# A graph network layer on one core: the window rows asked for earlier, five groups of source rows fetched by SyncE, more groups on ScalarE, narrower last blocks

## The chip, the cores and the metric

The kernel runs on one NeuronCore of one Trainium2 chip. The metric is the device time of one execution in microseconds. A run is timed three times; the median counts. One further execution is recorded by the hardware profiler, and all rows below come from such a record.

## The reference

12,500 nodes with 128 features each, 400,000 edges sorted by their destination, 32 features per edge. Cut to what matters:

```
h   = relu(layernorm(x))
pre = concat(h[src], h[dst], edge_attr) @ w1 + b1            # one row per edge
m   = relu(pre) @ w2 + b2
agg = segment_sum(m, dst)                                    # one row per node
gi, gh = agg @ w_ih + b_ih, h @ w_hh + b_hh
r, z = sigmoid(i_r + h_r), sigmoid(i_z + h_z)
n   = tanh(i_n + r * h_n)
out = x + (1 - z) * n + z * h
```

## The kernel before

w1 is split in three. `A = h @ w1[0:128]` and `B = h @ w1[128:256] + b1` are computed once per node and kept in DRAM; the node states also stay in SBUF, transposed, as `hT_all`. An edge then needs a row of `A` (by its source), a row of `B` (by its destination) and a product with the last 32 rows of w1.

**Groups and units.** The edges are cut into 391 groups (`k`) of eight tiles of 128 edges, 1024 edges each. A group is worked in two units, so the main loop runs over 782 units (`u`), and unit `u` emits for several groups at once: the product for unit `u + 3`, the addition for unit `u + 2`, the sum over destinations for unit `u`.

**The product (`pre`, L644).** Since the edges are sorted, a tile's destinations lie in a window of 32 nodes. `RW` is a tile of 128 rows: twice 32 window rows of `B`, and the edge weights; there are four of them (`RW[k % 4]`). `window_rows(k)` (L575) brings the two sets of 32 rows with two DMAs of SyncE. `L` holds the one-hot matrix of the places (made on VectorE, L545) and the edge features; `fetch(q)` brings it for two groups with two DMAs of SyncE, `L<-in_dstP` (L533, 256 KB, each of two source rows repeated for 32 partitions) and `L<-in_eaP` (L536, 256 KB). There are three `L` buffers.

**The source rows.** For most groups POOL gathers the rows of `A` into a buffer `G` with eight indirect DMAs (L152), as far ahead as 12 buffers allow. VectorE adds them to the product and applies the relu in one instruction (L668). For some groups, spread evenly, the sources are brought "by hand": `one_by_one` copies single columns of `hT_all` into `HE`, on ScalarE (L905, 24 groups) or on VectorE (L912, two columns per instruction, 26 groups), with node numbers loaded into registers (L899, 16 or 32 per load); TensorE multiplies them with w1a into the same sum (L655), and ScalarE does the relu (L675). `run_jobs` spreads the copies of a job evenly over the units between two groups.

**The sums.** `seg` (L688) adds the rows of one group by destination, `take` (L696) copies the sums, and after each block of 14 groups `node` computes the gates for 512 nodes; `last_node` does so for the last block, step by step in the last units.

**The order of the work** is written out by hand: each engine runs its instructions in the order in which the main loop emits them. A unit has four phases; `other(phase)` places the jobs and the small work. Of SyncE, a unit emits, if its number is even, the `fetch` of every second group; in phase 2 of an odd unit `window_rows(k + 3)`; besides these the stores of `B` (L237), the loads and stores of the node blocks (L703, L800) and index tiles (L107, L118). SyncE's DMAs take eight semaphores in turn.

Of the kernel before, what the change touches and what calls it, by code (L numbers as in the profile page):

```python
# [23 lines left out]
GRP = 4  # L24
# [5 lines left out]
V = 32  # L30
# [2 lines left out]

BP, BW = 14, 512
DMIN = 320
BLOCKS = [(BP * b, BP, BW) for b in range(27)] + [(378, 5, 256), (383, 8, 320)]
NB = len(BLOCKS)
NW = 27
LEAST = [DMIN] * 28 + [16]
QP = 2  # L40
W = 96
NT = -(-N // 128)
NFULL = N // 128
BAT = (4,) + (8,) * 11 + (NFULL - 92, 1)
RAW = 10
GBUFS = 12
BATCH = 512
AHEAD = 32
ROOM = V * (AHEAD - 2)
PLACE = 20  # L50
CH = PLACE * PAIR
LOAD = {"act": 16, "dve": 32}
PIECE = 128
STEP = {"act": 4, "dve": 8}
SPREAD = {"dve": 26, "act": 24}
START = {"dve": 16, "act": 4}
NR = 12672

H_AT = 16512
# [3 lines left out]
def tile_gnn(ctx: ExitStack, tc: tile.TileContext, x, src, srcT, dstT, dstP, eaT, eaP, w1, b1, w2T, b2,  # L63
# [25 lines left out]

    mode, order = {}, {m: [] for m in SPREAD}  # L90
    for m, n in SPREAD.items():
        lo, hi = START[m] // 2 + 2, NP - {"dve": 9, "act": 6}[m]
        for i in range(n):
            k = lo + int((i + 1) * (hi - lo) / n)
            while k in mode:
                k += 1
            mode[k] = m
            order[m].append(k)
# [75 lines left out]
    nc.vector.memset(brow, 0.0)  # L174
    b1b = const.tile([128, D], F32, name="b1b")
    base_d = at[96:97, :NP - 1]
    by_hand = [k for m in ("act", "dve") for k in order[m]]
    NJ = len(by_hand)
    zrow = const.tile([1, BW], BF16, name="zrow")
    nc.vector.memset(zrow, 0.0)  # L180
    RW = [const.tile([128, 2, D], F32, name=f"RW{i}") for i in range(4)]
# [556 lines left out]
    def node(b):  # L738
        w = BLOCKS[b][2]
        g0, xb, offs = block_start(b)  # L740
        pt = ps1.tile([128, 512], F32, name="nd")[:, :w]
        pd = ps1.tile([128, 512], F32, name="misc")[:, :w]
        nc.vector.tensor_copy(dcol[:2 * V, :len(offs)], sums[:, :len(offs), D])
        zero(pt)
        for i in range(len(offs)):
            sum_of(b, pt, offs, i)
        zero(pd)
        for i in range(len(offs)):
            degree_of(b, pd, offs, i)
        d = step_of(b)  # L750
        yield 1
        carry(b, TOT, pt, d)
        carry(b, DEG[0:1, :], pd[0:1, :], d)
        yield 1
        g = nc.tensor.value_load(blk_i[0:1, b:b + 1], min_val=0, max_val=N - w)
        hT = hT_all[:, bass.ds(g, w)]

        def gate(name, i, with_h, with_s):
            c = slice(i * D, (i + 1) * D)
            ci = slice(2 * D, 3 * D) if i == 3 else c  # L760
            pg = ps1.tile([128, 512], F32, name=name)[:, :w]
            nc.tensor.matmul(pg, brow[:, c], DEG[:, :w], start=True, stop=False)  # L762
            if with_h:
                nc.tensor.matmul(pg, whh_s[:, ci], hT, start=False, stop=not with_s)
            if with_s:
                nc.tensor.matmul(pg, w2ih[:, ci], TOT[:, :w], start=False, stop=True)  # L766
            return pg

        pr = gate("nd", 0, True, True)
        yield 1  # L770
        r = temp(w)
        nc.scalar.activation(r, pr, AF.Sigmoid)  # L772
        ph = gate("misc", 3, True, False)
        yield 1
        t = temp(w)
        nc.vector.tensor_tensor(t, r, ph, op=ALU.mult)
        pi = gate("nd", 2, False, True)
        yield 1
        nc.vector.tensor_tensor(t, t, pi, op=ALU.add)
        pz = gate("misc", 1, True, True)  # L780
        yield 1
        nc.scalar.activation(t, t, AF.Tanh)
        z = temp(w)
        nc.scalar.activation(z, pz, AF.Sigmoid)
        yield 1
        gv = nc.vector.value_load(blk_i[0:1, b:b + 1], min_val=0, max_val=N - w)
        q = r
        nc.vector.tensor_tensor(q, hT_all[:, bass.ds(gv, w)], t, op=ALU.subtract)
        yield 1
        nc.vector.tensor_tensor(q, q, z, op=ALU.mult)  # L790
        yield 1
        nc.vector.tensor_tensor(q, q, t, op=ALU.add)
        yield 1
        po = ps1.tile([128, 512], F32, name="nd")[:w // 4, :]
        for i in range(4):
            nc.tensor.transpose(po[:, i * D:(i + 1) * D], q[:, i::4], ident)
        yield 1
        nc.vector.tensor_tensor(xb, xb, po.rearrange("p (i f) -> p i f", i=4), op=ALU.add)
        yield 4 if b < NW - 1 else 1
        nc.sync.dma_start(out[bass.ds(g0, w), :].rearrange("(p i) f -> p i f", i=4), xb)  # L800

    def last_node():
# [16 lines left out]
            sum_of(b, pt, offs, i)  # L819
        yield  # L820
        carry(b, DEG[0:1, :], pd[0:1, :], d)
        for i in range(n - 4, n - 1):
            yield
            sum_of(b, pt, offs, i)
        yield

        def gate(pool, name, i, h_too):
            c = slice(i * D, (i + 1) * D)
            pg = pool.tile([128, 512], F32, name=name)[:, :w]
            nc.tensor.matmul(pg, brow[:, c], DEG[:, :w], start=True, stop=False)  # L830
            if h_too:
                ci = slice(2 * D, 3 * D) if i == 3 else c
                nc.tensor.matmul(pg, whh_s[:, ci], hT, start=False, stop=i == 3)
            return pg

        def finish(pg, i):
            nc.tensor.matmul(pg, w2ih[:, i * D:(i + 1) * D], TOT[:, :w], start=False, stop=True)

        pr = gate(ps1, "nd", 0, True)
        ph = gate(ps1, "misc", 3, True)  # L840
        yield
        pi = gate(ps2, "seg", 2, False)
        pz = gate(ps2, "pre", 1, True)
        yield
        sum_of(b, pt, offs, n - 1)
        carry(b, TOT, pt, d)
# [44 lines left out]
        return h_bytes[:, bass.ds(v - H_AT, 4)]  # L891

    def one_by_one(m, k):
        et = {"act": ET.Activation, "dve": ET.DVE}[m]
        r = by_hand.index(k)
        hand[k] = pj.tile([128, PAIR * 128], F32, name=f"HE_{m}")
        he = hand[k].bitcast(U8)
        for e0 in range(0, PAIR * 128, LOAD[m]):
            _, vals = nc.values_load_multi_w_load_instructions(  # L899
                at[r:r + 1, e0:e0 + LOAD[m]], engines=[et], min_val=H_AT, max_val=H_AT + 4 * (N - 1),  # L900
                skip_runtime_bounds_check_because="src holds numbers of nodes")
            if m == "act":
                for i, v in enumerate(vals):
                    e = e0 + i
                    nc.scalar.copy(he[:, e * 4:e * 4 + 4], column(v))  # L905
                    if i % STEP[m] == STEP[m] - 1:
                        yield
                continue
            if e0 % PIECE == 0:
                both = pj.tile([128, PIECE // 2, 4], U16, name="both")  # L910
            for i in range(0, LOAD[m], 2):
                nc.vector.scalar_tensor_tensor(both[:, (e0 % PIECE + i) // 2, :], column(vals[i + 1]),  # L912
                                               256.0, column(vals[i]), op0=ALU.mult, op1=ALU.add)
                if i % STEP[m] == STEP[m] - 2:
                    if (e0 + i + 2) % PIECE == 0:
                        p0 = e0 + LOAD[m] - PIECE
                        nc.vector.tensor_copy(  # L917
                            he[:, p0 * 4:(p0 + PIECE) * 4].rearrange("p (n c b) -> p n c b", c=2, b=4),
                            both.bitcast(U8).rearrange("p n (b c) -> p n c b", c=2))
                    yield  # L920

    jobs = {}
    for m, kl in order.items():
        start = START[m]
        for k in kl:
            end = 2 * k - 4
            jobs.setdefault(start, []).append((m, k, end - start))
            start = end
    live = {}

    PH = 4
# [26 lines left out]
    gathers(0)  # L958
    for q in range(3):
        fetch(q)  # L960
    for k in range(3):
        window_rows(k)


# [30 lines left out]
                    left.pop(0)  # L995

    last = last_node()
    LAST_STEPS = (NU - 8, NU - 6, NU - 5, NU - 4, NU - 2, NU - 1)

    for u in range(NU):  # L1000
        k, h = divmod(u, 2)
        gathers(u)
        if h == 0:
            if k % QP == 0:
                fetch(k // QP + 3)
            if k and k == BLOCKS[block(k)][0]:
                nodes_left.append([node(block(k) - 1), 2 if k < BLOCKS[-1][0] else 1])
            if k % PLACE == 1:
                indices(k // PLACE + 2)
            if k % PLACE == 5:  # L1010
                place(k // PLACE + 1)
                dst_tile(k // PLACE + 2)
            if k == NP - 20:
                check_windows()
        if u == min(START.values()) - 2:
            nc.vector.tensor_scalar(at[:NJ, :], at[:NJ, :], 4.0, float(H_AT), op0=ALU.mult, op1=ALU.add)

        def other(phase):
            run_jobs(u, phase)
# [1 line left out]
                batch_product(batch_due(k), wide[1], p3, "xb", 2)  # L1021
            if h == 1 and phase == 1 and batch_due(k):
                batch_store(batch_due(k))
            if h == 1 and phase == 2:
                window_rows(k + 3)
            if h == 0 and phase == 3:
                take(k - 1)
            if phase == 3:
# [11 lines left out]
        other(3)  # L1040
    for it, _ in nodes_left:
        run(it)
    next(last)
    next(last)
    take(NP - 1)
    run(last)

# [168 lines left out]
```

## Time and profile before

| What | Value |
|---|---|
| Median of 3 runs | 3548.33 us (3529.08 to 3559.73) |
| The profiled execution | 3567.68 us, its span 3565.9 us |
| Granted TensorE clock | 0.783 |
| TensorE busy | 2409.1 us (68%) |
| VectorE busy | 2266.0 us (64%) |
| ScalarE busy | 2661.4 us (75%) |
| POOL busy | 2614.4 us (73%) |
| Gathers from A on POOL | 2648 |
| SyncE: `RW<-B`, `L<-in_dstP`, `L<-in_eaP` | 782, 196 and 196 DMAs |
| DMA | 337.57 MB, mean 95 GB/s |

Busy time leaves out register loads, waits and the issuing of DMAs, so an engine may be occupied far more than its share says; SyncE shows none at all. A row of the waits names the instruction that waited, what it waited for, the total in us, the number of times and the longest. A row of a timeline gives the start, the length, the engine (a q behind it: its queue), line, operation, tiles and count, and in brackets the idle time before it. A row of a source view gives the smallest, median and largest duration in ns.

### The profile page before, as it was taken

The page shows a single profiled execution, that of the slowest core. Times are in us where ns is not written, and L with a number is a line of the kernel's source. Part 1 is how long each engine was busy: PE and PEld are TensorE (multiplying, and loading weights), DVE is VectorE, ACT ScalarE, POOL GpSimd, SP SyncE. Part 2 cuts the span into 40 slices and gives each one's busy share as a digit, 9 for nine tenths or more (in the row PEclk, how much of TensorE's full clock was granted, in tenths as well). Part 3 has the DMA queues.
Part 4 walks back from the last instruction along what each step waited for, and adds up shares of the span by engine and source line. Part 5 has one row for each costly group of instructions (what it writes and reads, how often), then busy time and mean ns, then how long its engine had stood idle before and what let it go on. Part 6 is the DMA issues. An engine that isn't in the chain of part 4 may idle for free. (4 is left out here: it accounts for less than half of the span.)

```text
span 3565.9 us, 80442 instructions
## 1 busy us (share of the span) xinstructions
PE 2409.1 (68%) x13224; PEld 1536.2 (43%) x13224; DVE 2266.0 (64%) x16484; ACT 2661.4 (75%) x25007; POOL 2614.4 (73%) x2734
## 2 busy tenths in 40 slices
PE   6567666675776676577667766765766676667768
PEld 6444444443444444344444443443444344434435
DVE  7656666666656666666566666666666666666664
ACT  5497778768777778787678688768876887796782
POOL 7677777777777777777777777777777777777770
PEclk8788877777777877777777878778777788787868
DMA  6433333333333333333333333333333333333431
GB/s 198 100 87 93 93 94 93 90 96 93 92 89 93 92 92 95 93 96 92 94 94 96 92 95 95 93 93 96 95 91 95 94 98 96 96 91 91 95 94 31
DMA packets 188489, 337.57 MB, mean 95 GB/s; under 512 B 65118, under 2 KB 108701, under 8 KB 187967
## 3 DMA queue, kind: packets, MB, share of 16 engines
q0 software_dynamic: 87200, 178.76, 21.5%
q1 hardware_dynamic: 100623, 153.56, 15.8%
q14 instruction: 412, 3.38, 0.3%
q8 instruction: 110, 1.80, 0.2%
q10 hardware_dynamic: 144, 0.07, 0.0%
HBM read 311.87 MB, written 20.27 MB: 93 GB/s over the span
## 5 line engine op out<-in xcount | busy, mean ns | idle before, releaser
L152 POOL DMA_INDIRECT G<-A,src_i x2648 | 2540.1, 959 | 839.6 <-issue 761.9
L905 ACT COPY HE_act<-hT_all 128x4 uint8 x24576 | 2470.3, 189 | 57.9 <-issue 38.3
L644 PE MATMUL pre<-RW,L 128*128 128x256 f32 x3128 | 1149.9, 495 | 1079.9 <-DMA RW<-B 827.5
L912 DVE SCALAR_TENSOR_TENSOR both<-hT_all 128x4 uint16 x13312 | 1138.0, 153 | 970.6 <-issue 961.4
L644 PEld LDWEIGHTS pre<-RW,L 128*128 128x128 f32 x3128 | 672.9, 240 | 1379.5 <-issue 669.8
L688 PE MATMUL seg<-RB,OH 128*32 128x129 f32 x6250 | 592.3, 319 | 0.0
L668 DVE CUSTOM_DVE_ANT_0 RB<-pre,G 128x512 f32<-128x512 f32 x662 | 448.5, 677 | 133.3 <-PE pre L644 98.8
L675 ACT ACTIVATE RB<-pre 128x512 f32<-128x512 f32 x120 | 70.7, 589 | 481.6 <-PE pre L655 481.3
L688 PEld LDWEIGHTS seg<-RB,OH 128*32 128x32 f32 x6250 | 326.8, 123 | 208.5 <-issue 159.0
L545 DVE TENSOR_SCALAR L<-L,node_of 64x512 f32<-64x512 int32 x383 | 187.2, 489 | 6.1 <-DMA L<-in_dstP 5.9
L772 ACT ACTIVATE gt<-nd 128x512 f32<-128x512 f32 (+1 forms) x28 | 16.5, 588 | 228.8 <-PE nd L766 228.8
L596 DVE TENSOR_TENSOR OH<-dloc,wide 128x256 f32<-128x256 f16 (+1 forms) x392 | 158.9, 406 | 0.5 <-issue 0.3
L696 DVE COPY sums<-seg 64x129 f32<-64x129 f32 x391 | 108.1, 277 | 17.2 <-PE seg L688 17.2
L683 PEld LDWEIGHTS <-zrow 1*64 1x64 bf16 x391 | 41.4, 106 | 143.4 <-issue 134.8
L683 PE MATMUL seg<-zrow 1*64 1x129 bf16 x391 | 99.4, 254 | 2.3 <-DVE sums L696 2.2
L917 DVE COPY HE_dve<-both 128x512 uint8<-128x512 uint8 x208 | 93.2, 448 | 7.1
L713 PE MATMUL nd<-spot,sums 64*128 64x40 f32 x766 | 94.2, 285 | 0.0
L713 PEld LDWEIGHTS nd<-spot,sums 64*128 64x128 f32 x766 | 90.7, 193 | 6.2 <-issue 6.1
L152 POOL DMA_INDIRECT G<-in_x,src_i x77 | 72.8, 945 | 24.4 <-issue 23.2
L655 PEld LDWEIGHTS pre<-w1a,HE_dve 128*128 128x128 f32 x416 | 75.6, 226 | 9.1
L655 PEld LDWEIGHTS pre<-w1a,HE_act 128*128 128x128 f32 x384 | 73.7, 239 | 9.1
L762 PE MATMUL nd<-DEG,brow 34*128 34x512 f32 (+1 forms) x112 | 75.0, 755 | 0.9 <-DVE DEG L727 0.9
(193 smaller groups left out, 1414.3 us busy)
## 6 DMA issues: line engine op xcount, KB each, us to landing
L<-in_dstP SPq DMA_DIRECT2D x195, 256.0 KB
L<-in_eaP SPq DMA_DIRECT2D x195, 256.0 KB
G<-A,src_i POOLq DMA_INDIRECT x2648
RW<-B SPq DMA_DIRECT2D x782, 16.0 KB
xb<-in_x SPq DMA_DIRECT2D x27, 256.0 KB
out<-xb SPq DMA_DIRECT2D x27, 256.0 KB
xs<-in_x SPq DMA_DIRECT2D x11, 512.0 KB
A<-asb SPq DMA_DIRECT2D x11, 512.0 KB
```

Of the source, the lines that this page charges most:

```text
L152: nc.gpsimd.indirect_dma_start(out=G[k][:, j, a, :], out_offset=None, in_=table, in_offset=bass.IndirectOffsetOnAxis(ap=src_i[c][:, i:i + ...
L545: nc.vector.tensor_scalar(o, i, node_of[:, k:k + 1], None, op0=ALU.is_equal)
L596: nc.vector.tensor_tensor(o, d.to_broadcast(shape), i.to_broadcast(shape), op=ALU.is_equal)
L644: nc.tensor.matmul(PP[u][:, 2 * i:2 * i + 2, :], Ls[k // QP][:, c0:c0 + 128], RW[k % 4], start=True, stop=not raw)
L655: nc.tensor.matmul(PP[u][:, 2 * i + a, :], cols, w1a, start=False, stop=n + 1 == len(l) or l[n + 1][1] != j)
L668: nc.vector._custom_dve(TENSOR_ADD_SAT, out=RB[u % 4][:, :, :D], in0=PP.pop(u), in1=unit(u), s0=float("inf"), s1=0.0)
L683: nc.tensor.matmul(SEG[k][:2 * V, :D + 1], zrow[:, :2 * V], zrow[:, :D + 1], start=True, stop=False)
L688: nc.tensor.matmul(SEG[k][V * a:V * (a + 1), :D + 1], OH[k][:, j, a, :], RB[u % 4][:, (j % 2) * 2 + a, :D + 1], start=False, stop=all(b != ...
L696: nc.vector.tensor_copy(sums[:, slot(block(k), k - BLOCKS[block(k)][0]), :], pm[:2 * V, :D + 1])
L713: nc.tensor.matmul(p[:, bass.ds(offs[i], V + SHIFT)], sums[:, slot(b, i), :D], spot, start=False, stop=i == len(offs) - 1)
L905: nc.scalar.copy(he[:, e * 4:e * 4 + 4], column(v))
L912: nc.vector.scalar_tensor_tensor(both[:, (e0 % PIECE + i) // 2, :], column(vals[i + 1]), 256.0, column(vals[i]), op0=ALU.mult, op1=ALU.add)
```

## The change

Four things are changed together.

1. `window_rows` is called for group `k + 4` at the start of the even unit, ahead of that unit's `fetch`, instead of for `k + 3` in phase 2 of the odd unit. Four groups instead of three are asked for before the loop.
2. Five groups get a new kind of job, `"sp"`: SyncE fetches their 1024 rows of `A` one by one, 512 bytes each, from addresses loaded into registers 32 at a time. The rows go into one buffer `G_sp`, and VectorE adds them as it adds gathered rows. A job ends eight units before its group and the next begins two units after that group's first. The numbers in `at` are turned into byte offsets of `A` for these groups, into offsets in `hT_all` for the others.
3. ScalarE gets 26 groups instead of 24; VectorE keeps 26. So 57 groups instead of 50 are not gathered by POOL. `G` has 11 buffers instead of 12.
4. The blocks at the end are cut otherwise (10, 9 and 8 groups, 384, 352 and 320 nodes wide, instead of 14, 5 and 8 groups of 512, 256 and 320), and `last_node` computes the parts of its gates that need no sums between the last units, one per step, instead of after them.

```diff
-BLOCKS = [(BP * b, BP, BW) for b in range(27)] + [(378, 5, 256), (383, 8, 320)]
+BLOCKS = [(BP * b, BP, BW) for b in range(26)] + [(364, 10, 384), (374, 9, 352), (383, 8, 320)]
-NW = 27
-LEAST = [DMIN] * 28 + [16]
+NW = 26
+LEAST = [DMIN] * 27 + [256, 128]
-GBUFS = 12
+GBUFS = 11
-ROOM = V * (AHEAD - 2)
+ROOM = V * (AHEAD - 4)
-LOAD = {"act": 16, "dve": 32}
+LOAD = {"act": 16, "dve": 32, "sp": 32}
-STEP = {"act": 4, "dve": 8}
-SPREAD = {"dve": 26, "act": 24}
-START = {"dve": 16, "act": 4}
+STEP = {"act": 4, "dve": 8, "sp": 4}
+ROW = 4 * D
+SPREAD = {"dve": 26, "act": 26, "sp": 5}
+START = {"dve": 16, "act": 4, "sp": 24}
...
     def one_by_one(m, k):
...
+        if m == "sp":
+            G[k] = pj.tile([128, GRP, 2, D], F32, name="G_sp", bufs=1)
+            rows = G[k].bitcast(U8)
...
+            if m == "sp":
+                for i, v in enumerate(vals):
+                    e = e0 + i
+                    a, j = divmod(e // 128, GRP)
+                    nc.sync.dma_start(rows[e % 128:e % 128 + 1, j, a, :],
+                                      A_bytes[bass.ds(v, ROW)].rearrange("(o f) -> o f", o=1))
+                    if i % STEP[m] == STEP[m] - 1:
+                        yield
+                continue
...
-            end = 2 * k - 4
+            end = 2 * k - (8 if m == "sp" else 4)
             jobs.setdefault(start, []).append((m, k, end - start))
-            start = end
+            start = end if m != "sp" else 2 * k + 2
...
-    for k in range(3):
+    for k in range(4):
         window_rows(k)
...
-    LAST_STEPS = (NU - 8, NU - 6, NU - 5, NU - 4, NU - 2, NU - 1)
+    LAST_STEPS = (NU - 8, NU - 6, NU - 5, NU - 4, NU - 3, NU - 2, NU - 1)
...
         if h == 0:
+            window_rows(k + 4)
             if k % QP == 0:
                 fetch(k // QP + 3)
...
-            if h == 1 and phase == 2:
-                window_rows(k + 3)
```

More of the change, by code (lines that the diff above doesn't have):

```diff
@@ L91, in tile_gnn @@
     for m, n in SPREAD.items():
-        lo, hi = START[m] // 2 + 2, NP - {"dve": 9, "act": 6}[m]
+        lo, hi = START[m] // 2 + 2, NP - {"dve": 9, "act": 6, "sp": 12}[m]
         for i in range(n):
@@ L176, in tile_gnn @@
     base_d = at[96:97, :NP - 1]
-    by_hand = [k for m in ("act", "dve") for k in order[m]]
+    by_hand = [k for m in ("sp", "act", "dve") for k in order[m]]
     NJ = len(by_hand)
+    place_of = const.tile([NJ, 2], F32, name="place_of")
+    for i, (to_sp, to_others) in enumerate(((ROW, 4), (0, H_AT))):
+        nc.vector.memset(place_of[:, i:i + 1], float(to_others))
+        nc.vector.memset(place_of[0:len(order["sp"]), i:i + 1], float(to_sp))
+    A_bytes = A.bitcast(U8).rearrange("n f -> (n f)")
     zrow = const.tile([1, BW], BF16, name="zrow")
@@ L798, in node @@
         nc.vector.tensor_tensor(xb, xb, po.rearrange("p (i f) -> p i f", i=4), op=ALU.add)
-        yield 4 if b < NW - 1 else 1
+        yield 4 if b < NW else 1
         nc.sync.dma_start(out[bass.ds(g0, w), :].rearrange("(p i) f -> p i f", i=4), xb)
@@ L821, in last_node, with gate @@
         carry(b, DEG[0:1, :], pd[0:1, :], d)
-        for i in range(n - 4, n - 1):
-            yield
-            sum_of(b, pt, offs, i)
         yield
-        def gate(pool, name, i, h_too):
+        def gate(pg, i, h_too):
             c = slice(i * D, (i + 1) * D)
-            pg = pool.tile([128, 512], F32, name=name)[:, :w]
             nc.tensor.matmul(pg, brow[:, c], DEG[:, :w], start=True, stop=False)
@@ L834, in gate, with bank @@
             return pg
+        def bank(pool, name):
+            return pool.tile([128, 512], F32, name=name)[:, :w]
         def finish(pg, i):
             nc.tensor.matmul(pg, w2ih[:, i * D:(i + 1) * D], TOT[:, :w], start=False, stop=True)
-        pr = gate(ps1, "nd", 0, True)
-        ph = gate(ps1, "misc", 3, True)
+        sum_of(b, pt, offs, n - 4)
+        pz = gate(pd, 1, True)
         yield
-        pi = gate(ps2, "seg", 2, False)
-        pz = gate(ps2, "pre", 1, True)
+        pr = gate(bank(ps1, "nd"), 0, True)
+        yield
+        sum_of(b, pt, offs, n - 3)
+        ph = gate(bank(ps1, "misc"), 3, True)
+        yield
+        sum_of(b, pt, offs, n - 2)
+        pi = gate(bank(ps2, "pre"), 2, False)
         yield
@@ L893, in one_by_one @@
     def one_by_one(m, k):
-        et = {"act": ET.Activation, "dve": ET.DVE}[m]
+        et = {"act": ET.Activation, "dve": ET.DVE, "sp": ET.SP}[m]
         r = by_hand.index(k)
-        hand[k] = pj.tile([128, PAIR * 128], F32, name=f"HE_{m}")
-        he = hand[k].bitcast(U8)
+        if m == "sp":
+            G[k] = pj.tile([128, GRP, 2, D], F32, name="G_sp", bufs=1)
+            rows = G[k].bitcast(U8)
+        else:
+            hand[k] = pj.tile([128, PAIR * 128], F32, name=f"HE_{m}")
+            he = hand[k].bitcast(U8)
         for e0 in range(0, PAIR * 128, LOAD[m]):
+            low, high = (0, ROW * (N - 1)) if m == "sp" else (H_AT, H_AT + 4 * (N - 1))
             _, vals = nc.values_load_multi_w_load_instructions(
-                at[r:r + 1, e0:e0 + LOAD[m]], engines=[et], min_val=H_AT, max_val=H_AT + 4 * (N - 1),
+                at[r:r + 1, e0:e0 + LOAD[m]], engines=[et], min_val=low, max_val=high,
                 skip_runtime_bounds_check_because="src holds numbers of nodes")
+            if m == "sp":
[5 more added lines that the diff above has]
+                    if i % STEP[m] == STEP[m] - 1:
+                        yield
+                continue
             if m == "act":
@@ L1015, in tile_gnn @@
         if u == min(START.values()) - 2:
-            nc.vector.tensor_scalar(at[:NJ, :], at[:NJ, :], 4.0, float(H_AT), op0=ALU.mult, op1=ALU.add)
+            nc.vector.tensor_scalar(at[:NJ, :], at[:NJ, :], place_of[:, 0:1], place_of[:, 1:2],
+                                    op0=ALU.mult, op1=ALU.add)
         def other(phase):
@@ L1042, in tile_gnn @@
         run(it)
-    next(last)
-    next(last)
     take(NP - 1)
```

## The prediction

> **What bounds the kernel now.** I read the waits of every engine first, then the costliest groups, then SyncE's own queue. The page's busy times, and four rows of the waits (engine, line, awaited thing, us in total, times, longest):
>
> ```profile
> PE 2409.1 (68%) x13224; PEld 1536.2 (43%) x13224; DVE 2266.0 (64%) x16484; ACT 2661.4 (75%) x25007; POOL 2614.4 (73%) x2734
> ...
> DVE both L912 <- issue: 961.4, 839, 2.9
> PE pre L644 <- DMA RW<-B: 827.5, 162, 10.1
> POOL G L152 <- issue: 785.1, 2576, 0.3
> DVE RB L668 <- PE pre L644: 98.8, 68, 5.0
> ```
>
> TensorE loses 827.5 us to the rows RW of the w1 product, but VectorE, which adds each product to the gathered rows, waits for the product only 98.8 us: it works on its own columns meanwhile. VectorE's 961.4 us "issue" is the loading of registers. POOL's idle time is 0.3 us behind each gather, so POOL issues without pause though it counts as busy 73%. The groups and the source views give the rates:
>
> ```profile
> L152 POOL DMA_INDIRECT G<-A,src_i x2648 | 2540.1, 959 | 839.6 <-issue 761.9
> L905 ACT COPY HE_act<-hT_all 128x4 uint8 x24576 | 2470.3, 189 | 57.9 <-issue 38.3
> L152 POOL DMA_INDIRECT G<-A,src_i x2648: 938/944/1601, 101.3 to 3478.2; - x190
> L533 SPq DMA_DIRECT2D L<-in_dstP x196: 549/568/646, 106.2 to 3518.5; - x196
> 145.40 0.62 SPq L533 DMA_DIRECT2D L<-in_dstP  x1
> ```
>
> A gather costs (3478.2 - 101.3) / 2648 = 1.275 us. L is fetched once in 4 units; the fetch at 145.40 us stands at unit 0, the last of 196 at unit 768, so 4 units take (3518.5 - 145.4) / 192 = 17.57 us, a unit 4.39 us. POOL, VectorE and TensorE's loop with RW stand close together. SyncE is not among them: in
>
> ```profile
> SPq L533 <- PE pre L644: 1959.9, 161, 18.5
> SPq L533 <- PE pre L655: 386.5, 32, 17.7
> SPq L575 <- DMA B<-xb: 213.0, 23, 10.7
> SPq L533 <- DMA L<-in_dstP: 40.7, 7, 7.4
> ```
>
> it waits 2346 us for TensorE to free an L buffer. The last row decides what follows. SyncE's DMAs use eight semaphores in turn, so each waits until the one issued eight before it has landed. The timeline of one fetch shows it:
>
> ```profile
> 1219.38 0.59 SPq L533 DMA_DIRECT2D L<-in_dstP  x1
> 1220.02 0.51 SPq L536 DMA_DIRECT2D L<-in_eaP  x1
> 1220.78 0.39 SPq L800 DMA_DIRECT2D out<-xb  x1
> 1221.29 0.86 SPq L575 DMA_DIRECT2D RW<-B  x2
> 1222.46 0.36 SPq L107 DMA_DIRECT2D src_i<-in_srcT  x1
> 1222.93 0.85 SPq L575 DMA_DIRECT2D RW<-B  x2
> SPq L533 <- DMA L<-in_dstP: 6.4, 1, 6.4
> ```
>
> Eight DMAs are issued by 1223.78; the ninth first waits 6.4 us for the first to land. So L<-in_dstP, issued at 1219.38, landed near 1230.2, 10.8 us later. Another such fetch,
>
> ```profile
> 2449.31 0.56 SPq L533 DMA_DIRECT2D L<-in_dstP  x1
> 2453.12 0.85 SPq L575 DMA_DIRECT2D RW<-B  x2
> SPq L533 <- DMA L<-in_dstP: 5.2, 1, 5.2
> ```
>
> gives 2453.97 + 5.2 - 2449.31 = 9.9 us. Today that is nearly free: 6 DMAs are issued in 17.57 us.
>
> Page rule: the Trainium skill's "DMA: Bandwidth & Descriptors" (Why a DMA increments its semaphore by 16 and not by 1) says that a SyncE transfer runs on the largest number of engines up to 16 that divides the slowest dimension of both sides, the lowest-numbered ones, so this broadcast from two source rows would run on two engines and a single row on one of those two. No view here names the engine; the 10 us for 256 KB agree with it, and the sum below would be the same.
>
> **The change part by part.**
>
> *SyncE's rows.* Five groups of 1024 rows, each row its own DMA; the jobs lie in units 24-166, 176-312, 322-458, 468-604 and 614-750, 686 units together, so 30 rows in 4 units. In the built program's order a fetch is followed by L<-in_eaP and 12 to 16 rows before the next RW, and each row waits for the semaphore of the DMA eight before. Hence, counted from a fetch: the fetch, L<-in_eaP and six rows go out, then SyncE stands until L<-in_dstP has landed, and 24 rows are still to come. The rows for their prices:
>
> ```profile
> L312 SPq DMA_DIRECT2D at<-in_src x50: 220/250/459, 17.4 to 33.6; - x50
> L575 SPq MOVE RW<-B x782: 29/29/43, 117.1 to 3526.8; - x196
> L568 SPq TENSOR_LOAD <-base_i x29: 737/1389/1647, 115.3 to 3488.0; - x29
> L701 SPq TENSOR_LOAD <-blk_i x29: 287/488/499, 276.2 to 3525.1; - x29
> 1415.80 1.95 SPq L575 DMA_DIRECT2D RW<-B  x4
> 1500.29 0.63 SPq L533 DMA_DIRECT2D L<-in_dstP  x1
> 1512.12 0.77 PE L644 MATMUL pre<-RW,L 128*128 128x256 f32 x1 [6.12 <-DMA RW<-B]
> 3502.32 0.64 SPq L533 DMA_DIRECT2D L<-in_dstP  x1
> 3511.74 0.77 PE L644 MATMUL pre<-RW,L 128*128 128x256 f32 x1 [5.30 <-DMA RW<-B]
> ```
>
> - A single-row DMA: 50 of them took 16.2 us with the same ring of eight, 0.33 us each; with the register move (0.03 and a gap as long) 0.36. Bounds 0.33 and 0.40.
> - Landing of L: 9.9 and 10.8 measured. RW behind L held TensorE until 11.8 us after a fetch at 1500.29, and until 9.4 us at 3502.32, when no gathers ran; taking the same 1.5 us off for RW's place behind L, L lands in about 7.9 us without gathers. With a fifth fewer gathers per us I take 9.8. Bounds 7.9 and 10.8.
> - A load of 32 registers: 1 value costs 0.488, 14 cost 1.389, so 32 about 2.6; 30/32 of one per cycle, of which a fifth falls into the stall: 2.0.
> - Four RW DMAs 2.0 (row at 1415.80: 1.95), other DMAs 0.3.
>
> Cycle of 4 units: 9.8 + 24 x 0.36 + 2.0 + 2.0 + 0.3 = 22.7 us, against 17.57. SyncE becomes the bound wherever it brings rows. What is late: RW for group k+4 and L stand behind the rows in SyncE's queue, so TensorE waits for RW, VectorE and ScalarE for products, POOL for buffers. The lead of five units only shifts the pipeline against SyncE; it cannot raise the queue's rate.
>
> *Rows five units ahead.* The RW pair moves from phase 2 of the odd unit to the start of the even one, ahead of that unit's fetch, and one group earlier. This removes most of the 827.5 us of TensorE, worth at most the 98.8 us of VectorE and what ScalarE's relu waits cost. It adds a wait: the four RW buffers make SyncE wait for the product of unit 2k+1, with the fetch behind it. TensorE runs that product in unit 2k-2, before SyncE comes there: nothing. Where SyncE sets the pace the whole gain is covered; nothing is counted.
>
> *56 gathers fewer.* 56 x 1.275 = 71.4 us off POOL; nothing while POOL is ahead of SyncE, all of it in a rival. Eleven buffers for twelve: the gathered rows lead by one group less; VectorE waited for a gather only 3.0 us:
>
> ```profile
> DVE RB L668 <- DMA G<-A,src_i: 3.0, 1, 3.0
> ACT RB L675 <- PE pre L655: 481.3, 56, 28.3
> ```
>
> *ScalarE 26 groups.* 2 x 1024 copies x 2470.3 / 24576 = 206 us more, under ScalarE's 481.3 us of waits for products; without that cover, 206 us.
>
> *Last blocks.* The gate products that stood between the last group and the last sum move ahead:
>
> ```profile
> 3548.72 0.78 PE L830 MATMUL nd<-DEG,brow 34*128 34x320 f32 x2
> 3552.91 0.81 PE L833 MATMUL pre<-hT_all,whh_s 128*128 x2
> 3553.65 0.41 PE L713 MATMUL wide<-spot,sums 64*128 64x40 f32 x2
> ```
>
> 3548.72 to 3553.65 is 4.9 us; I count 4.
>
> *Sum*, in the profiled execution's time. Before: 145.4 + 192 x 17.57 + 47.4 = 3565.9. After: 145.4 + 171.5 cycles x 22.7 = 3893 + the rest up to unit 768, 82 units, less 20 that the pipeline makes up in the four gaps between jobs (five units each), 62 x 4.39 = 272, + 47.4 - 4 = 4354. With 1.8 us around the span 4356; the profiled execution stands at 3567.68 against the median of 3548.33, a factor 0.9946: **4335 us**, 22% slower.
>
> Bounds: 7.9 + 24 x 0.33 + 4.3 = 20.1 us gives 3890; 10.8 + 24 x 0.40 + 4.8 (half a microsecond added for slower RW issues) = 25.2 us gives 4760.
>
> **The rivals.**
>
> *A: SyncE keeps up, POOL sets the end (faster).* If the ring never stalls, 4 units cost SyncE 30 x 0.36 + 2.5 + 2.0 + 1.1 + 0.3 = 16.7 us, under 17.57. Then POOL's last gather comes at 101.3 + 2592 x 1.275 = 3406, the same 87.7 us follow as after 3478.2, less 4: 3490, with 1.8 and the factor 3473. It decides as long as the stall is under 17.57 - 16.7 = 0.9 us: the fetch and seven DMAs behind it take 0.6 + 0.55 + 6 x 0.36 = 3.3 us to issue, so L would have to land within about 4.2 us. Against it: the stalls of 6.4 and 5.2 us after seven later DMAs. Page rule: the fit in "DMA: Bandwidth & Descriptors" (Anatomy of one DMA), about 2 us plus bytes over 436 GB/s, an estimate of 2.6 us for 256 KB, would bring this rival about; it is fitted on GpSimd's transfers, and the rows here say 9.9 and 10.8.
>
> *B: SyncE is the bound by its issue alone.* Without a stall, but with rows at 0.42 as for an RW DMA: 30 x 0.42 + 5.9 = 18.5 us, 3173 + 461 = 3634, median 3615. For it: two RW DMAs at 1221.29 took 0.86 us; against it the stalls.
>
> *C: rows land slowly.* If each row's landing takes 4 us beside the gathers, eight at a time, a row costs 0.5 us: 26.1 us, 4937, median 4910. For it: an RW DMA behind L took 11.8 us; against it: 0.33 us each in the 50 rows.
>
> *D: no change.* SyncE just keeps up and VectorE's own work (busy plus register loads) holds the pace: 3550.
>
> **How the numbers follow.** Main case 0.84, A 0.08, D 0.03, B 0.03, C 0.02. The range 3890 to 4760 is the main case with its bounds; 0.16 of the chance lies in the rivals and some of the main case beyond the bounds. Faster by over 1% (about what this kernel's measurement can tell from no change) 0.08, within 1% 0.03, slower 0.89.
>
> **What would show it.** Right: the L fetches about 22.7 us apart inside the jobs and under 18 outside them; SyncE waiting after a fetch some 6 us for DMA L<-in_dstP, hardly for PE; waits of TensorE for RW<-B or for L greater than 827.5 us; POOL's busy share well below 73%. Wrong: fetches 17 us apart inside the jobs, or L landing in under 4 us; then A holds. If the stall is there and the fetches are closer, the row price is mis-sized.

## The result, and the profile after

| | Kernel before | Kernel after |
|---|---|---|
| Median | 3554.03 us (4 runs, 3529.08 to 3570.09) | 4213.84 us (4 runs, 4211.44 to 4235.47) |
| Span of the profiled execution | 3565.9 us | 4209.6 us |
| Granted TensorE clock | 0.783 | 0.752 |

The ratio is 1.1869 (95% interval 1.1811 to 1.1926): 19% slower, where 22% had been forecast. In eight of the experiments below every kernel, the one before included, took about 5340 us or more, so a ratio is formed only within one set of runs, in which the kernel before ran too.

The page of after, its busy times and the row of the gathers (count, busy us, mean ns, idle us before them):

```profile
PE 2523.5 (60%) x13256; PEld 1604.5 (38%) x13256; DVE 2272.2 (54%) x16493; ACT 2876.9 (68%) x27059; POOL 2555.4 (61%) x2678
...
L153 POOL DMA_INDIRECT G<-A,src_i x2592 | 2481.1, 957 | 1529.8 <-issue 732.8
```

No engine is fuller than before; POOL falls from 73% to 61%, and a gather still takes 957 ns (959 before). The waits of after say what they all stand for (us in total, times, longest):

```profile
PE pre L650 <- DMA RW<-B: 1148.2, 215, 13.8
DVE both L936 <- issue: 988.4, 835, 2.4
...
ACT RB L681 <- PE pre L661: 728.3, 50, 46.4
POOL G L153 <- DVE RB L674: 709.0, 152, 24.6
DVE L L551 <- DMA L<-in_dstP: 598.3, 142, 9.0
```

TensorE's wait for RW, which the earlier request was to remove, grew from 827.5 to 1148.2 us. VectorE now waits 598.3 us for L, and POOL, which had waited 27.9 us in all for buffers that VectorE empties, waits 709.0 us for them. So two transfers are late, RW and L, and SyncE issues both. SyncE's own waits:

```profile
SPq L921 <- DMA L<-in_dstP: 904.2, 172, 7.8
SPq L921 <- DMA L<-in_eaP: 75.7, 163, 1.3
SPq L539 <- PE pre L650: 65.0, 32, 12.3
SPq L581 <- PE pre L650: 38.8, 19, 7.9
SPq L539 <- PE pre L661: 32.4, 8, 10.3
```

Before, the fetches of L waited 2346 us for TensorE. Now the rows (L921) wait 904.2 us for L<-in_dstP to land, 172 times, 5.3 us each, and for TensorE SyncE hardly waits (136 us in the last three rows). The timeline of SyncE from one fetch to the next inside a job, and one earlier stretch of rows that has no stall:

```profile
1505.31 5.10 SPq L921 DMA_DIRECT2D G_sp<-A  x16
...
3305.28 0.59 SPq L539 DMA_DIRECT2D L<-in_dstP  x1
3305.92 0.50 SPq L542 DMA_DIRECT2D L<-in_eaP  x1
3306.53 11.35 SPq L921 DMA_DIRECT2D G_sp<-A  x16
3317.98 0.81 SPq L581 DMA_DIRECT2D RW<-B  x2
3318.89 7.32 SPq L921 DMA_DIRECT2D G_sp<-A  x16
3326.38 0.81 SPq L581 DMA_DIRECT2D RW<-B  x2
3327.30 0.57 SPq L539 DMA_DIRECT2D L<-in_dstP  x1
```

Sixteen rows without a stall take 5.10 us. Behind the fetch they take 11.35, which is 6.25 more. SyncE's waits in this stretch give 5.2 us of that to the semaphore of L<-in_dstP, in one wait, and 0.5 to that of L<-in_eaP; the rest is not assigned. (The 7.32 us hold a register load.) The fetches are 22.02 us apart here. Over the whole trace I took the start of every fetch: 169 intervals inside the jobs have a mean of 21.93 us, 23 outside them 13.49 us. The source views give the rates and both ends of the loop:

```profile
L921 SPq DMA_DIRECT2D G_sp<-A x5120: 224/228/687, 259.0 to 4118.8; - x197
L914 SPq TENSOR_LOAD <-at x160: 1877/2142/2660, 256.6 to 4096.4; - x160
L539 SPq DMA_DIRECT2D L<-in_dstP x196: 557/587/762, 110.1 to 4163.3; - x196
```

169 x 21.93 + 23 x 13.49 = 4016 us from the fetch at unit 0 (146.2 us) to the last at 4163.3; before, 192 x 17.57 = 3373. The 643 us between them are the whole 643.7 us by which the span grew.

### The profile page after: what moved, and what is told of

Its sections match the earlier page's. It is cut to its first block, busy times and chain, and to the rows that moved or that the text cites. A ratio compares the mean times of both kernels' runs of the same rounds, so it can differ in the third digit from the quotient of the medians.

```text
span 4209.6 us, 93129 instructions
## 1 busy us (share of the span) xinstructions
PE 2523.5 (60%) x13256; PEld 1604.5 (38%) x13256; DVE 2272.2 (54%) x16493; ACT 2876.9 (68%) x27059; POOL 2555.4 (61%) x2678
## 3 DMA queue, kind: packets, MB, share of 16 engines
q0 software_dynamic: 85408, 175.09, 18.1%
## 5 line engine op out<-in xcount | busy, mean ns | idle before, releaser
L153 POOL DMA_INDIRECT G<-A,src_i x2592 | 2481.1, 957 | 1529.8 <-issue 732.8
L929 ACT COPY HE_act<-hT_all 128x4 uint8 x26624 | 2687.5, 189 | 58.1 <-issue 35.8
L650 PE MATMUL pre<-RW,L 128*128 128x256 f32 x3128 | 1209.3, 516 | 1609.7 <-DMA RW<-B 1148.2
L650 PEld LDWEIGHTS pre<-RW,L 128*128 128x128 f32 x3128 | 705.7, 252 | 1928.7 <-issue 820.7
L694 PE MATMUL seg<-RB,OH 128*32 128x129 f32 x6250 | 611.2, 327 | 0.0
L551 DVE TENSOR_SCALAR L<-L,node_of 64x512 f32<-64x512 int32 x383 | 190.4, 497 | 605.6 <-DMA L<-in_dstP 598.3
L674 DVE CUSTOM_DVE_ANT_0 RB<-pre,G 128x512 f32<-128x512 f32 x648 | 440.0, 679 | 130.6 <-PE pre L650 116.5
L778 ACT ACTIVATE gt<-nd 128x512 f32<-128x512 f32 (+2 forms) x28 | 16.4, 587 | 367.1 <-PE nd L772 367.0
L719 PE MATMUL nd<-spot,sums 64*128 64x40 f32 x766 | 112.3, 316 | 0.0
L719 PEld LDWEIGHTS nd<-spot,sums 64*128 64x128 f32 x766 | 108.6, 226 | 7.5 <-issue 7.5
L661 PE MATMUL pre<-w1a,HE_dve 128*128 128x128 f32 x416 | 81.1, 330 | 0.0
```

Of the source, the lines that this page charges most:

```text
L153: nc.gpsimd.indirect_dma_start(out=G[k][:, j, a, :], out_offset=None, in_=table, in_offset=bass.IndirectOffsetOnAxis(ap=src_i[c][:, i:i + ...
L551: nc.vector.tensor_scalar(o, i, node_of[:, k:k + 1], None, op0=ALU.is_equal)
L650: nc.tensor.matmul(PP[u][:, 2 * i:2 * i + 2, :], Ls[k // QP][:, c0:c0 + 128], RW[k % 4], start=True, stop=not raw)
L661: nc.tensor.matmul(PP[u][:, 2 * i + a, :], cols, w1a, start=False, stop=n + 1 == len(l) or l[n + 1][1] != j)
L674: nc.vector._custom_dve(TENSOR_ADD_SAT, out=RB[u % 4][:, :, :D], in0=PP.pop(u), in1=unit(u), s0=float("inf"), s1=0.0)
L694: nc.tensor.matmul(SEG[k][V * a:V * (a + 1), :D + 1], OH[k][:, j, a, :], RB[u % 4][:, (j % 2) * 2 + a, :D + 1], start=False, stop=all(b != ...
```

## The experiments

The theory to be tested: the rows cost what they cost because the ring of eight semaphores ties them to a slow L. It has rivals: that SyncE is full by issue alone, or that another part (the earlier RW, ScalarE's two groups, the last blocks) does the harm.

**L as two DMAs, rows and all else kept.** "Split L" gives each DMA one source row and 32 partitions, so the outermost dimension is 32 instead of 2; the 256 KB are the same.

```diff
-        nc.sync.dma_start(
-            Ls[q].bitcast(I32)[:2 * V, :n * 512],
-            bass.AP(tensor=p.tensor, offset=p.offset, ap=[list(p.ap[0]), [0, V], [1, n * 512]]))
+        for a in range(2):
+            nc.sync.dma_start(
+                Ls[q].bitcast(I32)[V * a:V * (a + 1), :n * 512],
+                bass.AP(tensor=p.tensor, offset=p.offset + a * p.ap[0][0], ap=[[0, V], [1, n * 512]]))
```

> The kernel of e2_split_L again (the changed kernel, L<-in_dstP cut into one DMA for each source row), since in the runs before this one the kernel before itself took 5360 us, with ScalarE and VectorE waiting 2113 and 1633 us for their own issue, so that SyncE was not the bound there. Where the kernel before takes about 3550 us: theory T expects 3400 to 3500 us, each half of L landing in 3 to 4 us and no long waits of SyncE for it; rival R1 (issuing 5120 rows is the cost) 3800 us or more.

Measured: 3419.95 us (3417.06 to 3424.75) against 3555.35, ratio 0.9633 (0.959 to 0.9676). This kernel is faster than the kernel before and the kernel after. A transfer's landing is read here from the last update of its semaphore ahead of the next DMA on it, and given as a median. Each half of L lands 2.85 us after its issue, and both have landed 3.4 us after the first was issued; the whole L of the kernel after takes 9.34 us. SyncE's timeline, its rows in the source view, and the waits of all engines:

```profile
1503.00 0.81 SPq L540 DMA_DIRECT2D L<-in_dstP  x2
1503.86 0.51 SPq L543 DMA_DIRECT2D L<-in_eaP  x1
1504.48 6.50 SPq L922 DMA_DIRECT2D G_sp<-A  x16
...
1519.95 0.79 SPq L540 DMA_DIRECT2D L<-in_dstP  x2
```

```profile
POOL G L153 <- issue: 760.0, 2492, 0.3
...
PE pre L651 <- DVE RB L675: 627.2, 320, 7.7
...
PE pre L651 <- DMA RW<-B: 163.9, 55, 7.2
```

```profile
L922 SPq DMA_DIRECT2D G_sp<-A x5120: 224/228/417, 246.3 to 3297.2; - x197
L153 POOL DMA_INDIRECT G<-A,src_i x2592: 940/944/1787, 103.2 to 3395.7; - x200
```

The same 5120 rows, at the same 228 ns of issue, now leave 16.95 us between two fetches (mean inside the jobs 17.21). The sixteen rows behind a fetch take 6.50 us instead of 11.35. POOL has again hardly a wait but the 0.3 us behind each gather and sets the pace, with (3395.7 - 103.2) / 2592 = 1.270 us a gather. With L early the earlier RW is in time too: TensorE's wait for it is 163.9 us. So neither the rows nor their issue cost the 660 us by themselves; the slow L ahead of them did.

What stands behind L also lands late, and not only its issue is held. In the kernel after, a row issued within 4 us of a fetch lands 8.0 us after its own issue (median), one issued 9 us or more behind it after 1.4 us; with the split the first of these is 2.7 us. No run changed the eight semaphores, so how much of the stall would stay without the ring is not shown.

**No row groups, L as it was.** The rest of the change (earlier RW, 26 groups on ScalarE, last blocks) stays. The second line taken out only prepared the rows' offsets.

```diff
-SPREAD = {"dve": 26, "act": 26, "sp": 5}
+SPREAD = {"dve": 26, "act": 26, "sp": 0}
...
-        nc.vector.memset(place_of[0:len(order["sp"]), i:i + 1], float(to_sp))
```

> The changed kernel without SyncE's rows (as e1_no_rows), L<-in_dstP still one DMA. Where the kernel before takes about 3550 us: theory T expects 3440 to 3510 us (POOL's 2632 gathers set the end, TensorE's wait for RW under 200 us); rival R2 (the earlier RW or ScalarE's two groups slow the kernel) 3600 us or more. Where it takes about 5350 us, with ScalarE's copies waiting over 2000 us for issue, ScalarE is the bound and this kernel tells only what ScalarE's two groups cost: 5500 to 5550 us.

Measured: 3471.37 us (3470.58 to 3471.89) against 3556.17, ratio 0.9747 (0.97 to 0.9795). Its gathers, and SyncE's waits:

```profile
L153 POOL DMA_INDIRECT G<-A,src_i x2632: 938/944/1724, 101.9 to 3450.5; - x188
```

```profile
SPq L538 <- PE pre L649: 1062.3, 159, 12.5
SPq L580 <- PE pre L649: 967.5, 169, 15.8
```

SyncE waits for TensorE again, now with RW too, and TensorE's wait for RW is down to 6.3 us. The rest of the change does no harm: it gains 2.5%. So the loss takes both, the rows and the slow L ahead of them; each without the other is faster than the kernel before. The source view says where the 2.5% lie. Before, the last gather came at 3478.2 and 87.7 us followed; here it comes at 3450.5 (16 gathers fewer) and only 19.1 us follow in a span of 3469.6. The kernel before was thus not held by POOL alone: the loop, which waited for RW, ended behind it, by an estimate of 87.7 / (2 x 4.39) = 10 groups, against two here (19.1 us). From this kernel to the one with split L and rows there are 40 gathers fewer, 40 x 1.270 = 51 us by the rate above; the spans differ by 3469.6 - 3419.5 = 50.1. So that is about what five groups of rows are worth once SyncE keeps up. (The two ran in different sets, with the kernel before at 3556.17 and 3555.35 us, and the kernel with split L and no rows was not run.)

**The kernel before, with split L alone** (the edit of the first experiment on the old kernel).

> The kernel before with L<-in_dstP cut into one DMA for each source row (as e9_before_split_L_again), where the kernel before takes about 3550 us. Theory T: RW was late because it stood behind the slow L; TensorE's wait for RW falls from 827.5 us to under 250 us and POOL's 2648 gathers set the end: 3470 to 3520 us. Rival: RW is late because it is asked late: wait above 500 us, time 3540 to 3560 us.

Measured: 3482.71 us (3479.89 to 3483.19) against 3566.68, ratio 0.9767 (0.9733 to 0.9802). Its waits and gathers:

```profile
PE pre L645 <- DVE RB L669: 800.2, 405, 7.1
POOL G L152 <- issue: 785.4, 2577, 0.3
...
PE pre L645 <- DMA RW<-B: 1.1, 2, 0.9
```

```profile
L152 POOL DMA_INDIRECT G<-A,src_i x2648: 940/944/1778, 102.5 to 3451.6; - x190
```

TensorE's 827.5 us for RW are down to 1.1, though RW is asked for as late as before: RW had been late because it stood behind L. Its landings agree: RW issued within 4 us of a fetch landed after 9.5 us in the kernel before and lands after 3.3 us here (medians); RW issued 9 us or more behind one takes under 1.9 us in both. 3481.1 - 3451.6 = 29.5 us follow the last gather instead of 87.7. So asking earlier (2.5%, with 16 gathers fewer and the new last blocks in it) and making L fast (2.3%) remove the same wait in two ways.

**Six row groups, with split L.** This loads SyncE's issue further while L stays fast.

```diff
-SPREAD = {"dve": 26, "act": 26, "sp": 5}
+SPREAD = {"dve": 26, "act": 26, "sp": 6}
```

> The kernel of e5_split_L_again with six groups of rows on SyncE instead of five (L in two DMAs), 36 rows in 4 units. With L landing early only SyncE's own issue is left: 36.4 rows x 0.32 + 1.14 loads x 2.14 + RW 1.8 + L 1.4 + short stalls 0.5 + other DMAs 0.3 = 18.1 us for 4 units, over the 16.8 that POOL needs. Theory T: SyncE is the bound again, 145 + 169 x 18.1 + 281 + 45 = 3530 us, slower than the 3420 with five. Rival: SyncE has room, and eight gathers fewer on POOL make it 10 us faster, 3410 us.

Measured: 3760.25 us (3753.53 to 3763.96) against 3566.68, ratio 1.0548 (1.0508 to 1.0588). The direction was as forecast, the size not. SyncE's waits, and its timeline from fetch to fetch:

```profile
SPq L922 <- DMA L<-in_eaP: 107.9, 117, 2.2
SPq L540 <- PE pre L651: 99.6, 24, 10.0
```

```profile
1507.95 0.81 SPq L540 DMA_DIRECT2D L<-in_dstP  x2
...
1517.64 8.61 SPq L922 DMA_DIRECT2D G_sp<-A  x20
1527.89 0.83 SPq L582 DMA_DIRECT2D RW<-B  x2
1528.82 0.81 SPq L540 DMA_DIRECT2D L<-in_dstP  x2
```

SyncE has no long wait for a landing and still needs 19.63 us between fetches (mean inside the jobs; 18.1 had been forecast). Its records sum, per cycle, to 8.5 us of row DMAs, 1.1 of their register moves, 2.5 of the loads of row addresses, 2.6 of RW and L issues, 0.8 of small instructions, 0.6 of waits for L<-in_eaP and some 3.6 of gaps between instructions. The gaps between two rows, about 2 us of the 3.6, are within the 0.32 us that the forecast has for a row; the other gaps were in none of its terms. This is the rival "full by issue alone", and it holds from the sixth group on; with five groups the cycle is 17.2 us, about POOL's pace.

**The same questions where ScalarE was the bound.** Eight further runs belong to sets in which the kernel before took about 5350 us. First set: no row groups; split L with five groups; split L on the kernel before; two row groups with L as it was (`"sp": 2`).

> The changed kernel without SyncE's rows: its five groups go back to POOL's gathers, all other parts of the change stay (RW asked five units ahead, ScalarE 26 groups, VectorE 26, narrower last blocks, 11 buffers). Theory T (SyncE's ring of eight stands behind L<-in_dstP, so the rows make SyncE the bound): without rows the fetches need only 6 DMAs in 4 units, the ring never closes, TensorE's wait for RW falls below 200 us, and POOL with 2632 gathers sets the end: 3480 to 3550 us. Rival R2 (what slows is the earlier RW, which now waits for TensorE in front of the fetch, or ScalarE's two groups): 3900 us or more.

> The changed kernel with one edit: L<-in_dstP is brought by two DMAs of 32 partitions, one for each of the two source rows, instead of one of 64. Theory T adds that L<-in_dstP is slow because its two source rows confine it to few DMA engines; cut so, each half should land in 3 to 4 us, SyncE's stall should fall from about 5 us per fetch to under 1, its cycle of 4 units to about 16 us, and POOL sets the end: 3400 to 3500 us. Rival R1 (issuing 5120 rows costs SyncE too much by itself): no more than the stall's share comes back, 3800 us or more.

> The kernel before with the same edit of L<-in_dstP alone. Theory T: RW, issued right behind L, lands in about 3 us instead of 9, TensorE's wait for RW falls from 827.5 us to under 250; the time falls only as far as POOL allows, 3480 to 3550 us. If the slow landing came from the bytes or the traffic and not from the shape, landing and time stay: 3540 to 3560 us.

> The changed kernel with two groups of rows on SyncE instead of five, spread over the same units, so about 12 rows in 4 units instead of 30. Theory T: a cycle costs SyncE 9.4 + 6 x 0.33 + 1.9 + 0.8 + 0.3 = 14.4 us, under the 17 us of the rest, so SyncE is no bound and the time falls to 3450 to 3560 us. Rival R1 (a cost in proportion to the rows: 660 us for five groups): 3770 to 3820 us.

| Kernel | us | before | ratio (95%) |
|---|---|---|---|
| No row groups | 5539.51 | 5360.49 | 1.0329 (1.0305 to 1.0353) |
| Split L, five groups | 5568.74 | 5360.49 | 1.039 (1.0368 to 1.0411) |
| Before, split L | 5354.26 | 5360.49 | 0.9987 (0.9971 to 1.0003) |
| Two row groups | 5568.77 | 5360.49 | 1.0399 (1.0369 to 1.0429) |

Three of the four were run again in such sets, two groups twice:

> The kernel of e1_no_rows again (the changed kernel without SyncE's rows, their five groups back on POOL; L<-in_dstP still one DMA), on a chip where the kernel before takes about 3550 us. Theory T: SyncE is no bound, TensorE's wait for RW falls below 200 us since RW is asked five units ahead, POOL's 2632 gathers set the end: 3440 to 3510 us. Rival R2 (the earlier RW or ScalarE's two groups slow the kernel): 3600 us or more.

> The kernel of e4_two_row_groups again (two groups of rows on SyncE instead of five, about 12 rows in 4 units; L<-in_dstP one DMA), where the kernel before takes about 3550 us. Theory T: a cycle of 4 units costs SyncE 9.4 + 6 x 0.33 + 1.9 + 0.8 + 0.3 = 14.4 us, under what POOL needs, so the stall behind L stays in the trace but costs nothing: 3430 to 3520 us. A cost in proportion to the rows (660 us for five groups): 3770 to 3820 us.

> The kernel before with L<-in_dstP cut into one DMA for each source row, RW still asked late, where the kernel before takes about 3550 us. Theory T: RW was late because it stood behind the slow L; now L lands in about 3 us and RW in about 2, TensorE's wait for RW falls from 827.5 us to under 250 us, and POOL's 2648 gathers set the end: 3470 to 3520 us, so that most of what the earlier RW brings comes without asking earlier. Rival: RW is late because it is asked late; then the wait stays above 500 us and the time at 3540 to 3560 us.

> The changed kernel with two groups of rows on SyncE instead of five (as e4_two_row_groups): about 12 rows in 4 units, L<-in_dstP one DMA. Where the kernel before takes about 3550 us, theory T: the stall behind L stays in the trace, but a cycle of 4 units costs SyncE only 9.4 + 6 x 0.40 + 1.9 + 0.8 + 0.3 = 14.8 us, under the 17 that POOL needs, so it costs nothing and two groups fewer on POOL than without rows count: 3440 to 3490 us. A cost in proportion to the rows (740 us for five groups against none): 3750 to 3790 us.

No row groups: 5523.57 against 5340.82, 1.034 (1.0306 to 1.0373). Two groups: 5567.77 against 5354.66, 1.0418 (1.0387 to 1.0449), and 5570.0 against 5358.68, 1.0392 (1.0364 to 1.042). Before with split L: 5350.55 against 5343.05, 1.0011 (0.9991 to 1.003). None of these times is the one expected where the kernel before takes about 3550 us, because another engine sets the pace. The row of ScalarE's copies in the kernel before with split L (first set), and in the one without rows:

```profile
L906 ACT COPY HE_act<-hT_all 128x4 uint8 x24576 | 2751.6, 190 | 2135.3 <-issue 2113.4 <-ACT HE_act L906 0.4
```

```profile
L928 ACT COPY HE_act<-hT_all 128x4 uint8 x26624 | 2964.6, 190 | 2176.6 <-issue 2155.5
```

A copy on ScalarE still takes 190 ns, but the copies wait 2113.4 us for their own issue where the first profile had 38.3. Copies and their idle time fill 4887 of 5337.8 us, and ScalarE's two further groups make it 5141 of 5540.5. Four units take 5350 / 782 x 4 = 27.4 us there, more than the 21.93 that SyncE needs. VectorE's own columns wait for their issue too, 1632.6 us in the first of the two kernels for 961.4 in the first profile. So these runs agree with the theory without testing it: SyncE's queue is hidden, split L gains nothing, and rows cost under 1% (at most 1.0418 against 1.0329). What they show is that the rest of the change costs about 3.3% when ScalarE is the bound; ScalarE's two groups are the part of it that adds to ScalarE. Why the two engines issued slowly in these sets is open. So is the dose of two row groups where the kernel before takes 3555 us; it was not measured there.

## Why the prediction was right

**The mechanism and its place.** Each sign that the prediction named is in the profile: fetches 21.93 us apart in the jobs (22.7 forecast) and 13.49 outside (under 18), a stall of 5.3 us for DMA L<-in_dstP (some 6), 65.0 + 38.8 + 32.4 us of waits for TensorE ("hardly"), 1148.2 us of TensorE's wait for RW (more than 827.5), POOL at 61% (well below 73%). That the slow L is the cause of the loss, and not only part of the picture, is shown by the kernel with split L: it differs in one transfer and takes 3419.95 us.

**The terms of the cycle.** The three that were estimated were all a little high. Landing of L: 9.34 us for 9.8. A row: 5.10 / 16 = 0.32 us for 0.36, under the lower bound of 0.33. A load of 32 registers: 2.14 us for 2.6. These take 0.5, 24 x 0.04 = 1.0 and 0.4 us off the 22.7; about 1.1 us come back through what the sum did not have, some 0.44 of it waits for L<-in_eaP (75.7 us in all), the rest gaps and small instructions. Net 0.77 us a cycle, times 171.5 = 132 of the 144 us by which the forecast span of 4354 exceeded 4209.6. The cycles were counted nearly right (169 for 171.5), and the 55 us that this takes off are mostly made up by the time outside the jobs, 310 us for 272. Part of the closeness of the number is therefore luck, since errors of both signs met. The factor 0.9946 has no counterpart either: the profiled execution of the kernel after (4211.44 us) is not longer than its median, so the factor took 0.5% off a forecast that was too high without a ground for it here.

The Trainium skill's "DMA: Bandwidth & Descriptors" (Why a DMA increments its semaphore by 16 and not by 1) has a transfer use the largest number of engines up to 16 that divides the slowest dimension of both sides: two for this broadcast, 16 for each half of the split one. The trace agrees in time: 9.34 us for the whole, 3.4 us for both halves. No view names the engines, but the records of the semaphores differ as well: most of the whole broadcasts leave three updates (165 of 196), most halves 16 (300 of 392). By the Trainium skill's "DMA: Bandwidth & Descriptors" (Anatomy of one DMA), a fit to transfers that GpSimd issues, an estimate for 256 KB is 2.6 us; only the split form comes near it.

**The earlier RW.** "Where SyncE sets the pace the whole gain is covered" was right for this kernel. The wait for TensorE that it adds came to 38.8 us on RW, near the forecast nothing. But its worth without that cover had been read from VectorE's 98.8 us and ScalarE's relu waits, and a better reading was in the quoted rows: most of the 87.7 us behind the last gather were a loop that lags. The tail fell by 87.7 - 19.1 = 68.6 us in the kernel without rows.

**The gathers.** 56 fewer were priced at 71.4 us, to be had only where SyncE keeps up. In the kernel after they gain nothing. In the kernel with split L the last gather comes 3478.2 - 3395.7 = 82.5 us earlier.

**ScalarE's groups.** Taken as covered by its waits for products: in the kernel without rows, which is 2.5% faster, they are. The price without cover was put at 206 us; about 180 us were measured where ScalarE was the bound (5539.51 - 5360.49 and 5523.57 - 5340.82), with the rest of the change in it.

**The last blocks.** 4 us were counted for gates moved ahead. From the last fetch to the end there are 46.3 us against 47.4, so 1 us of it is seen. The timeline of TensorE near the end shows the gates now between the sums:

```profile
4192.83 0.80 PE L832 MATMUL nd<-DEG,brow 34*128 34x320 f32 x2
...
4197.29 0.41 PE L719 MATMUL wide<-spot,sums 64*128 64x40 f32 x2
```

**The rivals.** A needed L to land within about 4.2 us. Split L makes it 3.4 for both halves, and A comes true: 3419.95 us where A gave 3473. Its POOL part was close (last gather at 3406 forecast, 3395.7 measured); its tail of 87.7 - 4 us was the mis-sized term, 23.8 measured. B's mechanism appears only once L is split and a sixth group is added. C fell: a row costs 0.32 us beside the gathers, and only the rows right behind a fetch land late. D fell with A's condition.

## What to carry to other kernels

Before adding many small DMAs to a queue that works in order and reuses a few semaphores, look for the slowest transfer in it: here a landing of 9.3 us stalled the queue for 5.3 us in every cycle, although only 256 KB moved, and what was issued right behind it landed late as well. Mend that transfer first, for instance by cutting a broadcast of two source rows into one DMA for each. And read how long the kernel runs on behind an engine's last instruction: an engine that never pauses is not the only bound if the loop behind it ends some ten groups later.

## What the runs showed that was not expected

- The slow L also held a neighbour that was not changed: L<-in_eaP, issued right behind it, landed 9.4 us after its issue in the kernel after and 4.0 us with split L (medians).
- The form of a DMA counted for more than its bytes: 256 KB in one DMA with an outermost dimension of 2 landed in 9.34 us, in two DMAs with 32 each in 3.4 us (2.85 us each). The split changes the count of DMAs along with the dimension; that the dimension alone does it was not tried.
- A register load on SyncE grows slower than by its values: 0.488 us for one, 1.389 for 14, 2.142 for 32.
- SyncE's gaps between instructions add up: some 3.6 of 19.63 us per cycle with six row groups.
- ScalarE's copies waited 38.3 us for their own issue in one set of runs and 2113.4 in another, for the same line of code and 190 ns each, while the kernel went from about 3555 to 5350 us. The cause was not found.
